# Pairwise bilinear interaction: transposes in feature pairs, x blocks by GpSimd's queue over 15 engines, and a last tile in six groups

## The chip, the cores and the metric

The kernel runs on one core of a Trainium2 chip. The metric is device time in microseconds (us) of one execution. TensorE (PE) multiplies, VectorE (DVE), ScalarE (ACT) and GpSimd (POOL) work elementwise, and SyncE (SP) only issues transfers. Sixteen DMA engines move data between device memory and the on-chip buffers; SP, ACT and POOL each put transfers on a queue of their own, and all three queues are served by the same sixteen engines.

## What is computed

There are 4096 batch rows, 32 features a row and 64 numbers a feature, all float32. For each of the 496 pairs of features i < j there is a 64 x 64 matrix. Feature i is multiplied by the pair's matrix, and the product elementwise by feature j:

```python
idx_i, idx_j = np.triu_indices(F, k=1)
vi = inputs[:, idx_i, :]
vj = inputs[:, idx_j, :]
vidots = jnp.einsum('bpd,pde->bpe', vi, W)
return vidots * vj
```

The output has 4096 x 496 x 64 numbers, 520 MB; x has 33.6 MB and w 8.1 MB.

## The kernel before

A *block* is 256 batch rows, two per partition; the 16 blocks give 32 *tiles* of 128 rows (`NB = 2` in a block). A tile's 496 pairs are cut into five *groups* (`bounds`, L45) of 90, 97, 99, 105 and 105 pairs. Each group is collected in an output buffer `ot` (three of them) and stored with one transfer on SP's queue (L266). A store has one row of up to 26,880 bytes per partition.

The multiplication needs x with the features' numbers on the partitions. `turn_x` (L138) makes a *run*: eight transposes on PE into a PSUM buffer, one of four, and one copy by ACT into `xT`. Transpose n takes the slots n and n + 1 of the block's buffer `xs`, so that feature n stands in the lower half of the partitions in one transpose and in the upper half in the next. There are four runs, or 32 transposes, per tile. Slot 0 of `xs` is a zero slot, written by a memset in `new_x` (L72).

The matrices are put in order (`order_w`) and transposed (`turn_w`) once, at the start, in chunks of 128 pairs; each chunk has a buffer `wT[c]` of its own. Two halves h of the output columns stand on two halves of the partitions, which is why each feature is wanted in both.

A *step* is one i and up to 16 of its j: for each half a matmul into a PSUM buffer (L244; two if the step crosses from one w chunk to the next), and one product. The product is DVE's (L261), or, for seven of the i, ACT copies PSUM to a buffer `tmp` (L258) and POOL multiplies (L259).

`sched` fixes the order of the steps: the first three tiles go group by group together, since w is still being prepared, and then tile after tile. Each engine works through its own instructions in program order. A run of transposes is placed `AHEAD` = 4 steps before its first use (L174 to L179).

The loads of x: blocks 0 and 1 at the start on SP's queue; block b + 1 at the seventh step of block b (`LATE`, L189 to L191). They wait until the buffer's old tile is done with. Most are one transfer on ACT's queue (`load_x`), which all sixteen DMA engines share. Blocks 4, 7, 10 and 13 (`loads[s] % 3 == 1`, L218) come by `load_fifteen` (L95): 120 of the 128 rows on POOL's queue in two transfers of half the features each, and the eight other rows on ACT's queue, five and three. After each of POOL's transfers stands a tiny one of a few bytes (`turn_engines`, L86)[...]. `turn_engines(5)` stands at the start and `turn_engines(11)` at the end (L270).

Of the kernel before, what the change touches and what calls it, by code (L numbers as in the profile page):

```python
# [8 lines left out]
F32 = mybir.dt.float32  # L9
# [3 lines left out]
def kernel(  # L13
# [16 lines left out]
    nc = tc.nc  # L30

    B, F, D = x.shape
    P = 128
    NB = 2
    assert 2 * D == P and B % (NB * P) == 0
    NBLK = B // (NB * P)
    NP = F * (F - 1) // 2
    E2 = D // 2
    BANK = 512
    CH = BANK // E2  # L40
    RUN = 2 * BANK // P
    p0 = [i * (F - 1) - i * (i - 1) // 2 for i in range(F)]


    bounds = [0, p0[3], p0[6] + CH, p0[11], p0[17], NP]  # L45
    groups = list(zip(bounds[:-1], bounds[1:]))
    cap = max(b - a for a, b in groups)

    aside = (1, 3, 5, 7, 9, 11, 13)

    cuts = [*range(0, NP, P), NP]
    wrows = list(zip(cuts[:-1], cuts[1:]))

    const = ctx.enter_context(tc.tile_pool(name="const", bufs=1))
    xpool = ctx.enter_context(tc.tile_pool(name="xpool", bufs=2))
    xtpool = ctx.enter_context(tc.tile_pool(name="xtpool", bufs=4))
    tpool = ctx.enter_context(tc.tile_pool(name="tpool", bufs=4))
    opool = ctx.enter_context(tc.tile_pool(name="opool", bufs=3))
    psum = ctx.enter_context(tc.tile_pool(name="psum", bufs=4, space=bass.MemoryType.PSUM))

    ident = const.tile([P, P], F32, tag="ident", name="ident")
    make_identity(nc, ident)

    xs = {}

    def rows_of(dram: bass.AP, blk: int) -> bass.AP:
        return dram[blk * NB * P : (blk + 1) * NB * P]

    def new_x(blk: int):

        xs[blk] = xpool.tile([P, 1 + NB * F, D], F32, tag="xs", name=f"xs_{blk}")
        nc.gpsimd.memset(xs[blk][:, 0, :], 0.0)  # L72

    def load_x(blk: int, eng, k0: int = 0, k1: int = NB):
        src = rows_of(x, blk).rearrange("(p k) f d -> p (k f) d", k=NB)
        eng.dma_start(out=xs[blk][:, 1 + k0 * F : 1 + k1 * F, :], in_=src[:, k0 * F : k1 * F, :])

# [3 lines left out]
    SWR = 120  # L81
# [4 lines left out]
    def turn_engines(k: int):  # L86
        n = k if k > 1 else 17
        c = used[0] % 8
        used[0] += 1
        src = x[: NB * n].rearrange("(p k) f d -> p k f d", k=NB)  # L90
        tc.keep_in_program_order(
            nc.gpsimd.dma_start(out=scratch[:n, :, c : c + 1], in_=src[:, :, 0, 0:1])  # L92
        )

    def load_fifteen(blk: int):  # L95
        rows = rows_of(x, blk).rearrange("(p k) f d -> p k f d", k=NB)
        dst = xs[blk][:, 1:, :].rearrange("p (k f) d -> p k f d", k=NB)
        for a, b in ((SWR, SWR + 5), (SWR + 5, P)):
            nc.scalar.dma_start(out=xs[blk][a:b, 1:, :], in_=rows[a:b].rearrange("p k f d -> p (k f) d"))
        for h in range(2):  # L100
            cut = slice(h * F // 2, (h + 1) * F // 2)
            tc.keep_in_program_order(
                nc.gpsimd.dma_start(out=dst[:SWR, :, cut, :], in_=rows[:SWR, :, cut, :])  # L103
            )
            turn_engines(1)


    wflat = w.rearrange("p d e -> p (d e)")
    raw, wT = {}, {}
    EU = 2 * BANK // P  # L110
    NU = E2 // EU

    def load_w(c: int, eng=nc.sync):

        a, b = wrows[c]
        pool, tag = ((opool, "ot"), (opool, "ot"), (const, "w3"), (const, "w3"))[c]
        raw[c] = pool.tile([P, D * D], F32, tag=tag, name=f"raw_{c}")
        eng.dma_start(out=raw[c][: b - a, :], in_=wflat[a:b])

    def order_w(c: int, k: int, copy):  # L120
        r = wrows[c][1] - wrows[c][0]
        rp = tpool.tile([P, EU, 2, D], F32, tag="tmp", name=f"rp_{c}_{k}")
        src = raw[c][:r, :].rearrange("p (d h e) -> p e h d", h=2, d=D)
        copy(rp[:r], src[:, k * EU : (k + 1) * EU])  # L124
        return rp

    def turn_w(c: int, k: int, rp, copy):
        r = wrows[c][1] - wrows[c][0]
        if c not in wT:
            wT[c] = const.tile([P, r, E2], F32, tag=f"w{c}", name=f"wT_{c}")  # L130
        pt = psum.tile([P, EU, P], F32, tag="ps", name=f"ptw_{c}_{k}")
        for n in range(EU):
            nc.tensor.transpose(  # L133
                pt[:, n, :r], rp[:r, n].rearrange("p h d -> p (h d)"), ident[:r, :r]
            )
        copy(wT[c][:, :, k * EU : (k + 1) * EU], pt[:, :, :r].rearrange("p e r -> p r e"))  # L136

    def turn_x(blk: int, k: int, q: int, copy):  # L138

        pt = psum.tile([P, RUN, P], F32, tag="ps", name=f"ptx_{blk}_{k}_{q}")  # L140
        for n in range(RUN):
            s = k * F + q * RUN + n
            nc.tensor.transpose(  # L143
                pt[:, n, :], xs[blk][:, s : s + 2, :].rearrange("p f d -> p (f d)"), ident
            )
        xT = xtpool.tile([P, RUN, P], F32, tag="xT", name=f"xT_{blk}_{k}_{q}")
        copy(xT, pt)  # L147
        return xT


    steps = [
        (g, i, c0, min(CH, F - 1 - i - c0))
        for i in range(F - 1)
        for c0 in range(0, F - 1 - i, CH)
        for g, (a, b) in enumerate(groups)
        if a <= p0[i] + c0 < b
    ]
    NS = len(steps)
    first = {}
    for s, (_, i, _, _) in enumerate(steps):  # L160
# [5 lines left out]
    NT = NBLK * NB  # L166
# [4 lines left out]
    place = {ts: n for n, ts in enumerate(sched)}  # L171


    AHEAD = 4  # L174
    due: dict = {}
    for t in range(NT):
        for q in range(F // RUN):
            at = place[t, first[q * RUN - 1] if q else 0] - AHEAD
            due.setdefault(max(0, at), []).append(("x", t // NB, t % NB, q))  # L179
    for c, orders, turns in (  # L180
# [9 lines left out]
    loads = {place[blk * NB, LATE]: blk + 1 for blk in range(2, NBLK - 1)}  # L190
# [12 lines left out]
    v, p, a = nc.vector.tensor_copy, nc.gpsimd.tensor_copy, nc.scalar.copy  # L203
    xT, rps = {}, {}
# [7 lines left out]
    ots = {}  # L212
    for s, (t, st) in enumerate(sched):
        blk, kt = divmod(t, NB)
        g, i, c0, m = steps[st]
        if s in loads:
            new_x(loads[s])
            if loads[s] % 3 == 1:  # L218
                load_fifteen(loads[s])
            else:  # L220
                load_x(loads[s], nc.scalar)
        for what, *args in due.get(s, ()):
            if what == "x":
                xT[tuple(args)] = turn_x(*args, a)
            elif what == "turn":
                turn_w(*args, rps.pop(tuple(args)), a)
            else:
                c, k = args
                rps[c, k] = order_w(c, k, (v, v, p, v)[c] if k % 2 == 0 else (v, v, p, a)[c])
                if (c, k) == (2, NU - 1):  # L230
                    load_w(3, nc.scalar)

        base, end = groups[g]
        pa = p0[i] + c0
        if pa == base:
            ots[t] = opool.tile([P, cap, D], F32, tag="ot", name=f"ot_{t}_{g}")
        ot = ots[t]
        ps = psum.tile([P, 2, CH, E2], F32, tag="ps", name=f"ps_{s}")
        for c, (lo, hi) in enumerate(wrows):
            lo, hi = max(pa, lo), min(pa + m, hi)  # L240
            if lo < hi:
                for h in range(2):
                    n = i + 1 - h
                    nc.tensor.matmul(  # L244
                        ps[:, h, lo - pa : hi - pa, :],
                        xT[blk, kt, n // RUN][h * D : (h + 1) * D, n % RUN, :],
                        wT[c][h * D : (h + 1) * D, lo - wrows[c][0] : hi - wrows[c][0], :],
                        start=True,
                        stop=True,
                    )  # L250
        o = pa - base
        j = 1 + kt * F + i + 1 + c0
        dst = ot[:, o : o + m, :].rearrange("p m (h e) -> p m h e", h=2)
        src = ps[:, :, :m, :].rearrange("p h m e -> p m h e")
        xj = xs[blk][:, j : j + m, :].rearrange("p m (h e) -> p m h e", h=2)
        if i in aside and c0 == 0 and s not in no_aside:
            tmp = tpool.tile([P, CH, 2, E2], F32, tag="tmp", name=f"tmp_{s}")
            nc.scalar.copy(tmp, src)  # L258
            nc.gpsimd.tensor_mul(dst, tmp, xj)  # L259
        else:  # L260
            nc.vector.tensor_mul(dst, src, xj)  # L261

        ends = (p0[2], end) if s < NS and (t, g) == (0, 0) else (end,)
        if pa + m in ends:
            n0 = p0[2] if len(ends) > 1 and pa + m == end else base
            nc.sync.dma_start(  # L266
                out=rows_of(out, blk).rearrange("(p k) n d -> p k n d", k=NB)[:, kt, n0 : pa + m, :],
                in_=ot[:, n0 - base : pa + m - base, :],
            )
    turn_engines(11)  # L270


# [25 lines left out]
```

## Time and profile before

| | |
|---|---|
| median of 9 runs (lowest, highest) | 1346.08 us (1345.64, 1346.99) |
| the profiled execution, its time | 1345.89 us |
| the profiled execution, its span, first to last instruction | 1344.1 us |
| busy: PE, DVE, ACT, POOL | 1166.7, 956.1, 374.0, 544.6 us |
| moved by DMA | 562.95 MB, mean 419 GB/s |
| queue of SP | 530.59 MB, 93.0% of sixteen engines' span |
| queue of ACT | 23.33 MB, 4.2% |
| queue of POOL | 7.88 MB, 1.5% |
| instruction fetches | 58 of 16 KB and 25 smaller packets, 0.3% |
| store of 105 pairs, issue to landing | 16.3 us (64 of them) |
| x load by ACT, issue to landing | 17.2 us (10) |
| x load by POOL, half of 120 rows, issue to landing | 31.4 us (8) |

The time outside the span is 1.77 us. A span is what the profile shows of one execution; the run's own time is what is compared between kernels. Busy shares are averages over the whole run, so a change in one stage has to be read from that stage.

### The profile page before, as it was taken

The numbers are of one execution on the slowest core, as the hardware profiler recorded it, in microseconds if no ns is written. First come the engines' busy times: TensorE is split into PE (matmuls) and PEld (weight loads), VectorE is DVE, ScalarE is ACT, GpSimd is POOL, SyncE is SP. The second block draws the span as 40 slices with busy tenths as digits, with TensorE's granted clock in tenths as the row PEclk, the third lists the DMA queues.
The fourth block names the chain that finished last, engine by engine and source line by source line (L and its number), as shares of the span: only waits on it lengthen the run. The fifth ranks groups of instructions, "written<-read, shape, count | busy, mean of one in ns | idle before, by whom it ended". The sixth has DMA issues, their size and how long they took to land.

```text
span 1344.1 us, 17902 instructions
## 1 busy us (share of the span) xinstructions
PE 1166.7 (87%) x7424; PEld 685.6 (51%) x7424; DVE 956.1 (71%) x1262; ACT 374.0 (28%) x367; POOL 544.6 (41%) x264
## 2 busy tenths in 40 slices
PE   6989889988799798888979988798988979988894
PEld 4555545544465454455545554454554545544552
DVE  4778767766677677776757777576776767767774
ACT  3442222323232232222322322222222323223321
POOL 1823434444243445333443534442444424344431
PEclk9989998999999899998989999899999999989997
DMA  9999999999999999999999999999999999999997
GB/s 378 370 431 424 424 428 433 428 417 430 422 431 422 426 430 407 426 422 430 429 424 420 411 425 430 420 428 419 421 419 415 428 427 427 421 433 421 421 414 320
DMA packets 28259, 562.95 MB, mean 419 GB/s; under 512 B 3457, under 2 KB 3457, under 8 KB 5505
## 3 DMA queue, kind: packets, MB, share of 16 engines
q1 hardware_dynamic: 24048, 530.59, 93.0%
q10 hardware_dynamic: 1632, 23.33, 4.2%
q0 software_dynamic: 2496, 7.88, 1.5%
q8 instruction: 58, 0.95, 0.3%
q14 instruction: 25, 0.20, 0.0%
HBM read 41.68 MB, written 520.09 MB: 418 GB/s over the span
## 4 chain that ended last, share of the span: by engine, by line
DMA 49%; PE 24%; DVE 17%; POOL 5%; issue 3%; ACT 1%; DVEq 0%; SPq 0%; POOLq 0%; ACTq 0%
DMA out_dram<-ot 48%; PE ps L244 19%; DVE ot L261 17%; POOL ot L259 4%; PE ptx L143 4%; PE ptw L133 1%; DMA raw<-in_L_rec_W_dram 1%; POOL scratch L92 1%; ACT tmp L258 0%; POOL xs L103 0%; DVE rp L124 0%; POOL rp L124 0%; DVEq L261 0%; ACT wT L136 0%; POOL xs L72 0%
## 5 line engine op out<-in xcount | busy, mean ns | idle before, releaser
L261 DVE TENSOR_TENSOR ot<-ps,xs 128x1024 f32<-128x1024 f32 (+15 forms) x1252 | 944.9, 808 | 355.9 <-DMA out_dram<-ot 185.0
L244 PE MATMUL ps<-wT,xT 64*128 64x512 f32 (+13 forms) x6272 | 1021.3, 469 | 125.0 <-DVE ot L261 113.8
L244 PEld LDWEIGHTS ps<-wT,xT 64*128 64x128 f32 x6272 | 558.1, 195 | 553.6 <-DVE ot L261 289.2
L259 POOL TENSOR_TENSOR ot<-tmp,xs 128x1024 f32<-128x1024 f32 x220 | 519.0, 2359 | 624.0 <-ACT tmp L258 453.3
L258 ACT COPY tmp<-ps 128x1024 f32<-128x1024 f32 x220 | 222.7, 1012 | 476.9 <-PE ps L244 433.0
L147 ACT COPY xT<-ptx 128x1024 f32<-128x1024 f32 x128 | 129.5, 1012 | 443.6 <-PE ptx L143 443.6
L143 PE MATMUL ptx<-ident,xs 128*128 128x128 f32 x1024 | 141.2, 281 | 30.7 <-DVE ot L261 21.9
L143 PEld LDWEIGHTS ptx<-ident,xs 128*128 128x128 f32 x1024 | 111.2, 142 | 76.9 <-issue 42.2
L72 POOL MEMSET xs<- 128x64 f32 x16 | 2.4, 151 | 147.3 <-DVE ot L261 147.3
L133 PE MATMUL ptw<-ident,rp 128*128 128x128 f32 (+1 forms) x128 | 19.3, 307 | 3.9 <-DVE rp L124 3.9
L133 PEld LDWEIGHTS ptw<-ident,rp 128*128 128x128 f32 (+1 forms) x128 | 16.3, 161 | 10.1 <-DVE rp L124 5.0
L136 ACT COPY wT<-ptw 128x1024 f32<-128x1024 f32 (+1 forms) x15 | 14.8, 984 | 21.1 <-PE ptw L133 18.2
L124 DVE COPY rp<-raw 128x1024 f32<-128x1024 f32 (+1 forms) x9 | 10.7, 1217 | 11.2 <-DMA raw<-in_L_rec_W_dram 11.2
L92 POOL DMA_DIRECT2D scratch<-in_r_inputs_dram x10 | 9.1, 908 | 0.2 <-issue 0.2
L124 POOL COPY rp<-raw 128x1024 f32<-128x1024 f32 x4 | 7.9, 1981 | 0.1
L124 ACT COPY rp<-raw 112x1024 f32<-112x1024 f32 (+1 forms) x3 | 5.9, 1959 | 4.3 <-POOL ot L259 2.5
L103 POOL DMA_DIRECT2D xs<-in_r_inputs_dram x8 | 6.0, 753 | 1.4 <-issue 1.4
L136 DVE COPY wT<-ptw 128x1024 f32<-128x1024 f32 x1 | 1.2, 1224 | 3.6 <-PE ptw L133 3.6
L147 ACT ACT_TABLE_LOAD x1 | 1.3, 1283 | 0.7 <-PEq L285 0.7
masks.py:197 POOL MEMSET ident<- 128x128 f32 x1 | 0.2, 205 | 0.3 <-POOLq L285 0.3
masks.py:199 POOL TENSOR_SCALAR_AFFINE_SELECT ident<-ident 128x128 f32<-128x128 f32 x1 | 0.3, 287 | 0.0
L285 POOL MEMSET const-float32-0.0<- 128x1 f32 x1 | 0.1, 93 | 0.3 <-issue 0.3
(3 smaller groups left out, 0.3 us busy)
## 6 DMA issues: line engine op xcount, KB each, us to landing
out_dram<-ot SPq DMA_DIRECT2D x64, 3360.0 KB, 16.3
out_dram<-ot SPq DMA_DIRECT2D x32, 3168.0 KB, 15.6
out_dram<-ot SPq DMA_DIRECT2D x32, 3104.0 KB, 17.0
out_dram<-ot SPq DMA_DIRECT2D x31, 2880.0 KB, 17.1
xs<-in_r_inputs_dram ACTq DMA_DIRECT2D x10, 2048.0 KB, 17.2
xs<-in_r_inputs_dram POOLq DMA_DIRECT2D x8, 960.0 KB, 31.4
raw<-in_L_rec_W_dram SPq DMA_DIRECT2D x3, 2048.0 KB, 17.3
xs<-in_r_inputs_dram SPq DMA_DIRECT2D x2, 1024.0 KB, 5.5
```

The source lines that it names most:

```text
L72: nc.gpsimd.memset(xs[blk][:, 0, :], 0.0)
L92: nc.gpsimd.dma_start(out=scratch[:n, :, c : c + 1], in_=src[:, :, 0, 0:1])
L103: nc.gpsimd.dma_start(out=dst[:SWR, :, cut, :], in_=rows[:SWR, :, cut, :])
L124: copy(rp[:r], src[:, k * EU : (k + 1) * EU])
L133: nc.tensor.transpose(pt[:, n, :r], rp[:r, n].rearrange("p h d -> p (h d)"), ident[:r, :r])
L136: copy(wT[c][:, :, k * EU : (k + 1) * EU], pt[:, :, :r].rearrange("p e r -> p r e"))
L143: nc.tensor.transpose(pt[:, n, :], xs[blk][:, s : s + 2, :].rearrange("p f d -> p (f d)"), ident)
L147: copy(xT, pt)
L244: nc.tensor.matmul(ps[:, h, lo - pa : hi - pa, :], xT[blk, kt, n // RUN][h * D : (h + 1) * D, n % RUN, :], wT[c][h * D : (h + 1) * D, lo - ...
L258: nc.scalar.copy(tmp, src)
L259: nc.gpsimd.tensor_mul(dst, tmp, xj)
L261: nc.vector.tensor_mul(dst, src, xj)
```

## The change

- `turn_x` makes four transposes per run rather than eight, each of two neighbouring features, and three copies by ACT: all four as they are, then each half of the partitions into the other half. A tile then has 16 transposes. The zero slot and its memset go. `xs` becomes one piece of 2048 numbers for each of the two rows with a gap of 16 numbers behind it.
- The first three w chunks share one buffer of 384 pairs, so a step that crosses pair 128 or 256 has one matmul per half.
- Runs are placed six steps before the first use of their features.
- `load_fifteen` is used for the blocks 3, 6, 9, 12 and 15. It sends 120 rows in one transfer of 8 KB pieces, then a tiny one, then the eight other rows in two transfers, all on POOL's queue.
- The last tile has six groups of 90, 97, 99, 55, 100 and 55 pairs. The fifth, of 100, is stored by POOL in two transfers, 120 rows and eight rows, with a gap of one pair between its halves of 50 in the output buffer. A tiny transfer `turn_engines(4)` follows it, in place of the one at the end.

```diff
-    RUN = 2 * BANK // P
+    RUN = 8
...
+    last = [*bounds[:4], p0[13] + CH, p0[21], NP]
+    last_groups = list(zip(last[:-1], last[1:]))
+    HALVED = 4
+    half = p0[17] - last[HALVED]
...
-        xs[blk] = xpool.tile([P, 1 + NB * F, D], F32, tag="xs", name=f"xs_{blk}")
-        nc.gpsimd.memset(xs[blk][:, 0, :], 0.0)
+        wide = xpool.tile([P, NB, F * D + 16], F32, tag="xs", name=f"xs_{blk}")
+        xs[blk] = wide[:, :, : F * D].rearrange("p k (f d) -> p k f d", d=D)
...
-        for a, b in ((SWR, SWR + 5), (SWR + 5, P)):
-            nc.scalar.dma_start(out=xs[blk][a:b, 1:, :], in_=rows[a:b].rearrange("p k f d -> p (k f) d"))
+        def part(ps: slice, fs: slice):
+            tc.keep_in_program_order(nc.gpsimd.dma_start(out=dst[ps, :, fs, :], in_=rows[ps, :, fs, :]))
+
+        part(slice(0, SWR), slice(0, F))
+        turn_engines(1)
         for h in range(2):
-            cut = slice(h * F // 2, (h + 1) * F // 2)
-            tc.keep_in_program_order(
-                nc.gpsimd.dma_start(out=dst[:SWR, :, cut, :], in_=rows[:SWR, :, cut, :])
-            )
-            turn_engines(1)
+            part(slice(SWR, P), slice(h * F // 2, (h + 1) * F // 2))
+
+    def store_fifteen(dram: bass.AP, ot: bass.AP):
+        dst = dram.rearrange("p (c n) d -> p c n d", c=2)
+        src = ot[:, : 2 * half + 2, :].rearrange("p (c n) d -> p c n d", c=2)[:, :, :half, :]
+        for rows in (slice(0, SWR), slice(SWR, P)):
+            tc.keep_in_program_order(nc.gpsimd.dma_start(out=dst[rows], in_=src[rows]))
...
-        if c not in wT:
-            wT[c] = const.tile([P, r, E2], F32, tag=f"w{c}", name=f"wT_{c}")
+        home, tag, n = (wrows[c][0], "w3", r) if c == 3 else (0, "w", wrows[3][0])
+        if home not in wT:
+            wT[home] = const.tile([P, n, E2], F32, tag=tag, name=f"wT_{home}")
...
-        pt = psum.tile([P, RUN, P], F32, tag="ps", name=f"ptx_{blk}_{k}_{q}")
-        for n in range(RUN):
-            s = k * F + q * RUN + n
+        pt = psum.tile([P, RUN // 2, P], F32, tag="ps", name=f"ptx_{blk}_{k}_{q}")
+        for u in range(RUN // 2):
+            f = q * RUN + 2 * u
             nc.tensor.transpose(
-                pt[:, n, :], xs[blk][:, s : s + 2, :].rearrange("p f d -> p (f d)"), ident
+                pt[:, u, :], xs[blk][:, k, f : f + 2, :].rearrange("p f d -> p (f d)"), ident
             )
-        xT = xtpool.tile([P, RUN, P], F32, tag="xT", name=f"xT_{blk}_{k}_{q}")
-        copy(xT, pt)
+        xT = xtpool.tile([P, 2, RUN // 2, P], F32, tag="xT", name=f"xT_{blk}_{k}_{q}")
+        copy(xT[:, 0], pt)
+        copy(xT[D:, 1], pt[:D])
+        copy(xT[:D, 1], pt[D:])
...
-    AHEAD = 4
+    AHEAD = 6
...
-            at = place[t, first[q * RUN - 1] if q else 0] - AHEAD
+            at = place[t, first[q * RUN]] - AHEAD
...
-            if loads[s] % 3 == 1:
+            if loads[s] % 3 == 0:
                 load_fifteen(loads[s])
...
-            nc.sync.dma_start(
-                out=rows_of(out, blk).rearrange("(p k) n d -> p k n d", k=NB)[:, kt, n0 : pa + m, :],
-                in_=ot[:, n0 - base : pa + m - base, :],
-            )
-    turn_engines(11)
+            dram = rows_of(out, blk).rearrange("(p k) n d -> p k n d", k=NB)[:, kt, n0 : pa + m, :]
+            if halved:
+                store_fifteen(dram, ot)
+                turn_engines(4)
+            else:
+                nc.sync.dma_start(out=dram, in_=ot[:, n0 - base : pa + m - base, :])
```

More of the change, by code (lines that the diff above doesn't have):

```diff
@@ L46 @@
     groups = list(zip(bounds[:-1], bounds[1:]))
+    last = [*bounds[:4], p0[13] + CH, p0[21], NP]
+    last_groups = list(zip(last[:-1], last[1:]))
+    HALVED = 4
+    half = p0[17] - last[HALVED]
+    assert last[HALVED + 1] == p0[17] + half
     cap = max(b - a for a, b in groups)
+    assert 2 * half + 1 < cap
     aside = (1, 3, 5, 7, 9, 11, 13)
@@ L69, in new_x @@
     def new_x(blk: int):
-        xs[blk] = xpool.tile([P, 1 + NB * F, D], F32, tag="xs", name=f"xs_{blk}")
-        nc.gpsimd.memset(xs[blk][:, 0, :], 0.0)
+        wide = xpool.tile([P, NB, F * D + 16], F32, tag="xs", name=f"xs_{blk}")
+        xs[blk] = wide[:, :, : F * D].rearrange("p k (f d) -> p k f d", d=D)
     def load_x(blk: int, eng, k0: int = 0, k1: int = NB):
-        src = rows_of(x, blk).rearrange("(p k) f d -> p (k f) d", k=NB)
-        eng.dma_start(out=xs[blk][:, 1 + k0 * F : 1 + k1 * F, :], in_=src[:, k0 * F : k1 * F, :])
+        src = rows_of(x, blk).rearrange("(p k) f d -> p k f d", k=NB)
+        eng.dma_start(out=xs[blk][:, k0:k1], in_=src[:, k0:k1])
     SWR = 120
@@ L96, in load_fifteen @@
         rows = rows_of(x, blk).rearrange("(p k) f d -> p k f d", k=NB)
-        dst = xs[blk][:, 1:, :].rearrange("p (k f) d -> p k f d", k=NB)
-        for a, b in ((SWR, SWR + 5), (SWR + 5, P)):
-            nc.scalar.dma_start(out=xs[blk][a:b, 1:, :], in_=rows[a:b].rearrange("p k f d -> p (k f) d"))
-        for h in range(2):
-            cut = slice(h * F // 2, (h + 1) * F // 2)
-            tc.keep_in_program_order(
-                nc.gpsimd.dma_start(out=dst[:SWR, :, cut, :], in_=rows[:SWR, :, cut, :])
-            )
-            turn_engines(1)
+        dst = xs[blk]
+        def part(ps: slice, fs: slice):
+            tc.keep_in_program_order(nc.gpsimd.dma_start(out=dst[ps, :, fs, :], in_=rows[ps, :, fs, :]))
+        part(slice(0, SWR), slice(0, F))
+        turn_engines(1)
+        for h in range(2):
+            part(slice(SWR, P), slice(h * F // 2, (h + 1) * F // 2))
[4 more added lines that the diff above has]
+            tc.keep_in_program_order(nc.gpsimd.dma_start(out=dst[rows], in_=src[rows]))
     wflat = w.rearrange("p d e -> p (d e)")
@@ L135, in turn_w, with steps_of @@
             )
-        copy(wT[c][:, :, k * EU : (k + 1) * EU], pt[:, :, :r].rearrange("p e r -> p r e"))
+        o = wrows[c][0] - home
+        copy(wT[home][:, o : o + r, k * EU : (k + 1) * EU], pt[:, :, :r].rearrange("p e r -> p r e"))
     def turn_x(blk: int, k: int, q: int, copy):
-        pt = psum.tile([P, RUN, P], F32, tag="ps", name=f"ptx_{blk}_{k}_{q}")
-        for n in range(RUN):
-            s = k * F + q * RUN + n
+        pt = psum.tile([P, RUN // 2, P], F32, tag="ps", name=f"ptx_{blk}_{k}_{q}")
+        for u in range(RUN // 2):
+            f = q * RUN + 2 * u
             nc.tensor.transpose(
-                pt[:, n, :], xs[blk][:, s : s + 2, :].rearrange("p f d -> p (f d)"), ident
+                pt[:, u, :], xs[blk][:, k, f : f + 2, :].rearrange("p f d -> p (f d)"), ident
             )
-        xT = xtpool.tile([P, RUN, P], F32, tag="xT", name=f"xT_{blk}_{k}_{q}")
-        copy(xT, pt)
-        return xT
[L151 to L157, printed above, removed]
+        xT = xtpool.tile([P, 2, RUN // 2, P], F32, tag="xT", name=f"xT_{blk}_{k}_{q}")
+        copy(xT[:, 0], pt)
+        copy(xT[D:, 1], pt[:D])
+        copy(xT[:D, 1], pt[D:])
+        return xT
+    def steps_of(groups):
+        return [
+            (g, i, c0, min(CH, F - 1 - i - c0))
+            for i in range(F - 1)
+            for c0 in range(0, F - 1 - i, CH)
+            for g, (a, b) in enumerate(groups)
+            if a <= p0[i] + c0 < b
+        ]
+    steps, last_steps = steps_of(groups), steps_of(last_groups)
     NS = len(steps)
@@ L214 @@
         blk, kt = divmod(t, NB)
-        g, i, c0, m = steps[st]
+        g, i, c0, m = (last_steps if t == NT - 1 else steps)[st]
         if s in loads:
             new_x(loads[s])
-            if loads[s] % 3 == 1:
+            if loads[s] % 3 == 0:
                 load_fifteen(loads[s])
@@ L231 @@
                     load_w(3, nc.scalar)
-        base, end = groups[g]
+        base, end = (last_groups if t == NT - 1 else groups)[g]
+        halved = (t, g) == (NT - 1, HALVED)
         pa = p0[i] + c0
@@ L238 @@
         ps = psum.tile([P, 2, CH, E2], F32, tag="ps", name=f"ps_{s}")
-        for c, (lo, hi) in enumerate(wrows):
-            lo, hi = max(pa, lo), min(pa + m, hi)
+        for lo, hi in ((0, wrows[3][0]), wrows[3]):
+            home, lo, hi = lo, max(pa, lo), min(pa + m, hi)
             if lo < hi:
                 for h in range(2):
-                    n = i + 1 - h
                     nc.tensor.matmul(
                         ps[:, h, lo - pa : hi - pa, :],
-                        xT[blk, kt, n // RUN][h * D : (h + 1) * D, n % RUN, :],
-                        wT[c][h * D : (h + 1) * D, lo - wrows[c][0] : hi - wrows[c][0], :],
+                        xT[blk, kt, i // RUN][h * D : (h + 1) * D, (i + h) % 2, i % RUN // 2, :],
+                        wT[home][h * D : (h + 1) * D, lo - home : hi - home, :],
                         start=True,
@@ L250 @@
                     )
-        o = pa - base
-        j = 1 + kt * F + i + 1 + c0
+        o = pa - base + (halved and pa - base >= half)
+        j = i + 1 + c0
         dst = ot[:, o : o + m, :].rearrange("p m (h e) -> p m h e", h=2)
         src = ps[:, :, :m, :].rearrange("p h m e -> p m h e")
-        xj = xs[blk][:, j : j + m, :].rearrange("p m (h e) -> p m h e", h=2)
+        xj = xs[blk][:, kt, j : j + m, :].rearrange("p m (h e) -> p m h e", h=2)
         if i in aside and c0 == 0 and s not in no_aside:
```

## The prediction

> **What bounds the kernel now.** I read the page's slices and queues first, then the stages, the waits, the end of the DMA, and the groups by shape.
>
> ```profile
> DMA  9999999999999999999999999999999999999997
> GB/s 378 370 431 424 424 428 433 428 417 430 422 431 422 426 430 407 426 422 430 429 424 420 411 425 430 420 428 419 421 419 415 428 427 427 421 433 421 421 414 320
> ...
> 33.00:100.00 67.00, 63.48 (x400) 38.61 (x398) 50.17 (x55) 29.29 (x28) 34.57 (x16) 0.95 0.97 400
> 100.00:1300.00 1200.00, 1057.91 (x6762) 617.53 (x6760) 870.03 (x1163) 325.89 (x322) 494.47 (x234) 0.96 1.00 424
> 1300.00:1345.00 45.00, 23.81 (x157) 14.43 (x154) 20.16 (x30) 6.08 (x6) 11.58 (x6) 0.78 0.79 335
> ```
>
> The last three lines are stages: length, busy PE, PEld, DVE, ACT and POOL, clock, DMA share, GB/s. Between 100 and 1300 us the 16 DMA engines are full; only the first 100 and the last 45 us are not. Bytes cannot be saved, so what can move is idle DMA time.
>
> ```profile
> DVE ot L261 <- DMA out_dram<-ot: 185.0, 84, 5.8
> POOL xs L72 <- DVE ot L261: 147.3, 14, 18.3
> ...
> 1318.81 7.86 DVE ot L261 x13
> 1326.67 0.13 DVEq L294
> ```
>
> The waits (total us, times, longest): VectorE waits 185.0 us for output buffers, 5.8 us a batch tile, so the multiplications are ahead of the DMA. The chain's end: the last group of 105 pairs is multiplied in 7.86 us and done at 1326.8.
>
> ```profile
> DMA  7079702220202000200020020002000000000000
> GB/s 323 0 323 1075 323 0 108 108 108 0 108 0 108 0 0 0 108 0 0 0 108 0 0 108 0 0 0 108 0 0 0 0 0 0 0 0 0 0 0 33
> ```
>
> This is the DMA view of 1334 to 1344 us, a slice each 0.25 us (a piece counts where it starts). From 1336 on one 26,880-byte piece starts about every microsecond: a single engine works alone. The packet records give the times: 13 engines finish the last store by 1336.0, others at 1336.8 and 1337.6, one at 1342.0; the span ends 2.1 us later. Sorted by store, the completions show this one engine, the laggard, 2.4 us behind at 178 us and 5 to 7 us behind through most of the later run. It falls back about 2.5% of the time, and catches up only while GpSimd loads x on 15 engines (7.2 to 3.5 us behind over the load at 517).
>
> Counting at each moment how many engines have no packet: 2.0 us before the first packet, 3.9 at 20 to 75 us, 5.9 between 100 and 1336 (2.5 of it after 1200), and 7.7 at the end, 5.6 of them waiting for the laggard. The idle time between 100 and 1336 comes when the laggard is over about 5.5 us late: it holds the output buffer that the next group needs.
>
> [...] a 26,880-byte piece takes 996 ns, 27.0 GB/s an engine, 432 for 16. [...] Here one stands out, and it falls back also when GpSimd transfers nothing. [...] this trace shows 5.4 us (issue 265.5, first 4 KB piece 270.9).
>
> **The change, part by part.**
>
> *Loads.* The packets cost 159 ns for 4 KB, 309 for 8 KB, 611 for 16 KB. A block loaded by ScalarE puts 8 x 611 = 4.89 us on each engine. Now: five blocks by GpSimd, 16 x 309 = 4.94 on 15 engines, and eight rows as 32 pieces of 4 KB over all 16, 0.32 each. Before: four blocks, 32 x 159 = 5.09 on 15 engines, none on the laggard[...]. Mean over engines: before 12 x 4.89 + 4 x 5.08 = 79.0 us, after 11 x 4.89 + 5 x 4.95 = 78.5: -0.4. Relief of the laggard against the others: before 4 x 5.09 = 20.4 us, after 5 x 4.94 = 24.7.
>
> What the laggard lost before is 20.4 (relief) + 6.2 (late at the end) + about 5.7 (the others idled) = 32 us, 6.05 per 246 us. After, the lag before each load (187, 431, 676, 923, 1169 us) should be 2.4, 3.5, 4.6, 5.7, 6.8, each load taking 4.9. Only the last two peaks pass 5.5, so of the 5.9 us about 1.2 stay: **-4.2**, keeping 0.5 for idleness of other causes (bounds -6 and 0).
>
> *Zero slot gone.* 16 memsets of 151 ns go. POOL's 147.3 us of waits stood before them with POOL otherwise idle; the load itself now waits for the same release, on ACT or POOL. Nothing. On POOL five blocks issue four DMAs each instead of four blocks with four (0.75 to 0.97 us each): 3.5 us once more, covered by POOL's 624 us idle; without cover the next product waits at most that.
>
> *Transposes and copies.*
>
> ```profile
> L258 ACT COPY tmp<-ps 128x1024 f32<-128x1024 f32 x220 | 222.7, 1012 | 476.9 <-PE ps L244 433.0 <-POOL ot L259 38.6
> L147 ACT COPY xT<-ptx 128x1024 f32<-128x1024 f32 x128 | 129.5, 1012 | 443.6 <-PE ptx L143 443.6
> L143 PE MATMUL ptx<-ident,xs 128*128 128x128 f32 x1024 | 141.2, 281 | 30.7 <-DVE ot L261 21.9 <-DMA xs<-in_r_inputs_dram 6.4
> ...
> L136 ACT COPY wT<-ptw 128x896 f32<-128x896 f32 x4 | 3.6, 906 | 8.9 <-PE ptw L133 5.9 <-DVE ot L261 2.9
> ```
>
> A run of eight transposes takes 1.09 us on PE; four take 0.55, so -70 us of PE in all, -2.2 a tile. ACT copies 1024 columns in 1012 ns and 896 in 906, so 512 in about 590; three are 1.76 us for one of 1.01: +0.75 a run, +96 in all, +3.0 a tile. Behind them on ACT stand copies into tmp, and POOL's products behind those. ACT idles over two thirds of the time and VectorE has 5.8 us a tile in hand, so in the middle this costs nothing. Six steps ahead instead of four leaves room for 1.76 us. The shared w buffer drops 256 matmul records at two crossings, same columns: nothing.
>
> In the first 75 us PE is the bound (95% busy from 33 to 100), and the 3.9 us of idle DMA is its. The three runs there before the first stores lose 1.6 us of PE, against 2.2 us more on ACT. I take **-1** (bounds -2.5 and +1.5).
>
> Fewer PE instructions mean fewer fetches (58 of 16 KB, 0.97 us each): -0.3 an engine. Loads, fetches and the tail's smaller pieces: **-0.7**.
>
> *The last tile*, on the clock of before, for the engines that lead. Pairs 90, 97, 99, then 55, 100 (GpSimd), 55. The lag there: 1.9 left after 1182, +3.2, about 5.1 instead of 6.4. Group 2 is transferred by 1319.2, the 55 by 1323.4 (14,080-byte rows, 8 in 4.2 us). The 100 pairs reuse the buffer of the 97, free on the leaders at 1311.5, on the laggard 5.1 later; nine products at about 0.8 us are 7.6 us, so done at 1324.8. GpSimd's store then needs 2.1 us (the tiny transfer at 1317.6 to its first packet) to 5.4 us (240 descriptors, as the loads); I take 5.4: 1330.2. The last 55 pairs are multiplied by 1329 and leave 0.85 us later (SP's first store: 27.64 to 28.48). So the leaders stand idle 1323.4 to about 1330, then have 4.2 + 7.7 us, seven of them one row of 0.95 us more: 1343.0. The laggard, relieved of seven of eight rows, is done near 1335. Against 1342.0: **+1** (bounds -2.5 and +2). That the new GpSimd transfers replace the closing tiny one is free: it was off the end.
>
> *Sum:* -4.2 -1 -0.7 +1 = -4.9 us. The profiled execution took 1345.89 (span 1344.12 and 1.77 around it); it lies 0.2 under the median, 1346.08. Forecast **1341.0**; own range 1339 to 1343.4.
>
> **Rivals.** Faster still: the last store starts after 2.1 us instead of 5.4 and the early runs pay fully, 3 to 4 us more: 1337.5. For it: HBM and the engines are idle then. Against it: the four loads all took about 5.4.
>
> No change: the idle time in the middle is not the laggard's but the group's own chain (release, 7 to 8 us of products, issue), and stays; with the tail's +1 and the other -1.7, near 1345. For it: stalls at 100 to 110 us, where the lag is small. Against it: under 0.1 us idle from 150 to 450, where the lag was mostly below 5.5.
>
> Slower: the three copies hold one of four PSUM buffers and ACT's queue, and PE and VectorE stop behind them. It decides once a run costs over 1.45 us of the chain (5.8 a tile in hand, four runs), more with PE's 0.55 back: about 2. That needs the half-width copies to cost a full 1.01 us each. Past it, each 0.1 us a run is 0.4 a tile and 13 us over 32 tiles; 0.35 a tile past it gives 11 - 5 = +6, 1352. Against: the slope of ACT's two widths.
>
> **How the numbers follow.** Forecast 0.42, faster still 0.22, no change 0.21, slower 0.15. A measurement of this kernel tells about 0.2% (2.7 us) from no change, so faster is 0.64, same 0.21, slower 0.15. The range 1335.5 to 1348.5 leaves out the slower case and a little of the fastest.
>
> **What would show it.** Right: the lag under 5.5 us until 900 us, idle engines under 2 us between 100 and 1300; no engine alone at the end, but a dip of all of them ahead of GpSimd's store; transposes 512, ACT copies near 590 ns. Wrong: the lag as large as before (the 15 engines are others), first GpSimd packets of the last store within 3 us, or VectorE's waits for the DMA gone and waits for PE or ACT in their place.

## The result and the profile after

The changed kernel takes 1355.04 us (median of 9 runs, 1352.88 to 1357.53), the kernel before 1346.23 in all its runs so far: ratio 1.0066, 95% interval 1.0057 to 1.0074. It is slower by 8.8 us, where 4.9 us less was forecast. The profiled execution took 1355.35 us with a span of 1353.6.

The page of the changed kernel, its slices and its DMA queues:

```profile
DMA  9999999999999999999999999999999999999995
GB/s 374 377 429 422 409 426 430 424 427 431 426 428 426 424 433 422 431 422 434 424 417 425 423 429 426 424 420 410 434 420 433 427 425 417 414 428 432 428 422 163
...
q1 hardware_dynamic: 24176, 527.31, 91.8%
q10 hardware_dynamic: 2576, 20.71, 3.8%
q0 software_dynamic: 2384, 13.78, 2.9%
```

The middle looks as before. The last slice fell from 320 to 163 GB/s. The stages of the same kernel (length; busy PE, PEld, DVE, ACT, POOL; clock; DMA share; GB/s) show what happens in it:

```profile
100.00:1300.00 1200.00, 1044.89 (x6076) 551.96 (x6072) 868.20 (x1164) 414.05 (x561) 495.38 (x224) 0.94 1.00 425
1320.00:1326.00 6.00, 5.82 (x38) 3.38 (x36) 4.90 (x6) 1.74 (x3) 0.82 (x2) 0.91 0.14 58
1326.00:1336.00 10.00, 2.57 (x24) 1.50 (x20) 3.19 (x9) 0.00 (x0) 1.12 (x2) 0.77 0.98 216
1336.00:1352.00 16.00, 0.00 (x0) 0.00 (x0) 0.00 (x0) 0.00 (x0) 0.00 (x0) 0.50 0.59 183
```

Two things are to be seen. From 1320 to 1326 us the DMA engines have almost nothing to do (share 0.14). That was in the forecast. From 1326 to 1336 they are all at work (0.98), yet move 216 GB/s, half of the 425 that the same share gives in the middle. That was not. In the packet records GpSimd's 12,800-byte pieces of the fifth group take 945 ns (median), many between 940 and 1000. At the 27 GB/s an engine of every other store (26,880 bytes in 996 ns) they would take 479 ns, and some do: eight of the 124 that started before 1334.4 us, and many of the later ones. That 15 engines carry the 120 rows is seen in the semaphore records of that transfer: of its 16 landing marks one comes at 1327.4 us, 0.9 us after the first piece starts, and the other fifteen from 1339.3 us on.

The end of the chain and GpSimd's own timeline:

```profile
1314.71 0.30 DVE ot L282
...
1324.00 5.06 DVE ot L282 x10
1329.06 0.13 DVEq L316
...
1310.24 2.34 POOL L280 TENSOR_TENSOR ot<-tmp,xs 128x1024 f32<-128x1024 f32 x1 [0.63 <-ACT tmp L279]
1325.18 1.35 POOL L118 DMA_DIRECT2D out_dram<-ot  x2 [12.60 <-DVE ot L282]
1326.53 0.59 POOL L99 DMA_DIRECT2D scratch<-in_r_inputs_dram  x1
```

VectorE is done with everything at 1329.1; the last piece lands at 1351.0. So 22 us of transfers stand after the last product, where the kernel before had 15 (1326.8 to 1342.0).

The groups on ScalarE and PE, for the copies that the change multiplied:

```profile
L163 ACT COPY xT<-ptx 128x512 f32<-128x512 f32 x128 | 74.9, 585 | 330.7 <-PE ptx L159 330.7
L159 PE MATMUL ptx<-ident,xs 128*128 128x128 f32 x512 | 85.7, 291 | 11.2 <-DMA xs<-in_r_inputs_dram 8.6
L165 ACT COPY xT<-ptx 64x512 f32<-64x512 f32 x128 | 74.5, 582 | 1.5
L164 ACT COPY xT<-ptx 64x512 f32<-64x512 f32 x128 | 73.9, 577 | 1.5
```

They cost what was worked out, 580 ns each and 94 us more in all than the one copy of before, and VectorE still waits for output buffers above all:

```profile
DVE ot L282 <- DMA out_dram<-ot: 204.7, 94, 6.3
```

So nothing here points to the copies. When I count the moments at which an engine has no packet, the middle even gained: between 100 and 1320 us 3.5 us of idleness instead of 5.8. The store of the 97 pairs of the last tile is through on the leading engines at 1307.3 us instead of 1311.5, that of the 99 at 1314.9 instead of 1319.7.

### The profile page after: what moved, and what is told of

The parts are those of the page before. It is cut to its first block, busy times and chain, and to the rows that moved or that the text cites. A ratio compares the mean times of both kernels' runs of the same rounds, so it can differ in the third digit from the quotient of the medians.

```text
span 1353.6 us, 16680 instructions
## 1 busy us (share of the span) xinstructions
PE 1149.1 (85%) x6656; PEld 611.6 (45%) x6656; DVE 954.6 (71%) x1262; ACT 467.6 (35%) x623; POOL 544.4 (40%) x254
## 4 chain that ended last, share of the span: by engine, by line
DMA 55%; PE 23%; DVE 12%; POOL 4%; issue 2%; ACT 1%; SPq 0%; DVEq 0%; POOLq 0%; ACTq 0%
DMA out_dram<-ot 53%; PE ps L265 21%; DVE ot L282 12%; POOL ot L280 4%; PE ptx L159 2%; DMA xs<-in_r_inputs_dram 2%; ACT tmp L279 1%; PE ptw L147 1%; DVE rp L137 0%; POOL rp L137 0%; ACT xT L163 0%; ACT xT L164 0%; DVEq L282 0%; POOL xs L107 0%; ACT xT L165 0%
## 5 line engine op out<-in xcount | busy, mean ns | idle before, releaser
L265 PE MATMUL ps<-wT,xT 64*128 64x512 f32 (+13 forms) x6016 | 1056.2, 492 | 163.7 <-DVE ot L282 158.5
L265 PEld LDWEIGHTS ps<-wT,xT 64*128 64x128 f32 x6016 | 540.2, 197 | 619.8 <-DVE ot L282 365.2
L163 ACT COPY xT<-ptx 128x512 f32<-128x512 f32 x128 | 74.9, 585 | 330.7 <-PE ptx L159 330.7
L159 PE MATMUL ptx<-ident,xs 128*128 128x128 f32 x512 | 85.7, 291 | 11.2 <-DMA xs<-in_r_inputs_dram 8.6
L159 PEld LDWEIGHTS ptx<-ident,xs 128*128 128x128 f32 x512 | 54.8, 143 | 85.4 <-DVE ot L282 59.4
L165 ACT COPY xT<-ptx 64x512 f32<-64x512 f32 x128 | 74.5, 582 | 1.5
L164 ACT COPY xT<-ptx 64x512 f32<-64x512 f32 x128 | 73.9, 577 | 1.5
L107 POOL DMA_DIRECT2D xs<-in_r_inputs_dram x15 | 9.5, 636 | 0.0
L99 POOL DMA_DIRECT2D scratch<-in_r_inputs_dram x7 | 6.2, 890 | 0.3 <-issue 0.3
```

What stands on the lines that cost most here:

```text
L107: tc.keep_in_program_order(nc.gpsimd.dma_start(out=dst[ps, :, fs, :], in_=rows[ps, :, fs, :]))
L159: nc.tensor.transpose(pt[:, u, :], xs[blk][:, k, f : f + 2, :].rearrange("p f d -> p (f d)"), ident)
L163: copy(xT[:, 0], pt)
L164: copy(xT[D:, 1], pt[:D])
L165: copy(xT[:D, 1], pt[D:])
L265: nc.tensor.matmul(ps[:, h, lo - pa : hi - pa, :], xT[blk, kt, i // RUN][h * D : (h + 1) * D, (i + h) % 2, i % RUN // 2, :], wT[home][h * ...
```

## The experiments

My new theory (A): the last tile costs more than the whole loss, and the rest gains. Within it, theory P: the rows are at fault. A store that is cut by rows runs at about half the rate (here 216 of 425 GB/s), whatever its queue and the number of its engines. That is a guess from these two figures; what in the hardware would do it, no run shows. Rivals: the loss is in the copies, the w buffer or the loads (B), in GpSimd's queue (Q), or in transfers over 15 engines as such (R).

**The last tile undone.** The changed kernel with five groups in the last tile, all by SP, and the closing tiny transfer back at the end:

```diff
-        g, i, c0, m = (last_steps if t == NT - 1 else steps)[st]
+        g, i, c0, m = steps[st]
...
-        base, end = (last_groups if t == NT - 1 else groups)[g]
-        halved = (t, g) == (NT - 1, HALVED)
+        base, end = groups[g]
...
```

> The changed kernel with the last tile as before: five groups, all stored by SP, the closing tiny transfer at the end. Theory A (the last tile costs all of the loss; loads, transposes and w buffer gain about 4.8 us, as the stores up to the last tile's third show): about 1341 us, the laggard alone at the end, 6 us late. Theory B (three copies by ACT, shared w buffer or the loads lose time as well): 1347 us or more.

1342.53 us (10 runs), ratio to before 0.9974 (0.9965 to 0.9984): 3.6 us faster than before. The view of its DMA from 1330 to 1340 us, a slice each 0.25 us, has the single late engine again:

```profile
DMA  7099702520022002000200020002000000000000
GB/s 323 0 753 645 323 0 108 215 108 0 0 108 108 0 0 108 0 0 0 108 0 0 0 108 0 0 0 108 0 0 0 0 0 0 0 0 0 0 0 33
```

Theory A holds: against this kernel the new last tile costs 12.5 us. The gain of the rest is a little under what was expected.

**The last tile alone.** The kernel before, with only the six groups and GpSimd's two transfers added:

> The kernel before with only the new last tile (six groups, the 100 pairs by GpSimd, 120 and 8 rows). Theory A: 12 to 15 us over before, 1358 to 1361 us, 12,800-byte pieces near 950 ns. Theory B: under 1350.

1358.61 us (4 runs), ratio 1.0094 (1.0079 to 1.0109): +12.5 us. Its 12,800-byte pieces took 948 ns (median). Nothing else of the change is needed for the loss.

**Six groups, all by SP.** The changed kernel, with the fifth group as an ordinary store:

```diff
-            if halved:
-                store_fifteen(dram, ot)
-                turn_engines(4)
-            else:
-                nc.sync.dma_start(out=dram, in_=ot[:, n0 - base : pa + m - base, :])
+            nc.sync.dma_start(out=dram, in_=ot[:, n0 - base : pa + m - base, :])
+    turn_engines(11)
```

> The changed kernel with the six groups kept and the group of 100 pairs stored by SP in one transfer of 128 rows. If the six groups alone leave the engines idle for some 7 us ahead of the 100 pairs, and the rest of the loss is GpSimd's store: 1341 to 1344 us, pieces of 25,600 bytes at about 950 ns. If the six groups are the whole loss: 1353 to 1355.

1343.27 us (20 runs), ratio 0.9978 (0.9971 to 0.9985). The six groups do leave the engines idle before the fifth (4.5 us between 1320 and 1336, averaged over the engines), but it hardly tells: 0.7 us over the five groups, within the intervals. In the gap the late engine catches up, so that at the end all 16 finish within 0.9 us instead of one 6.3 us late. The loss lies in the store itself.

**128 rows by GpSimd.** The changed kernel, with one transfer for the fifth group (here and in the next two the closing tiny transfer is `turn_engines(11)` instead of 4; it stands behind the store):

```diff
-        for rows in (slice(0, SWR), slice(SWR, P)):
-            tc.keep_in_program_order(nc.gpsimd.dma_start(out=dst[rows], in_=src[rows]))
+        tc.keep_in_program_order(nc.gpsimd.dma_start(out=dst, in_=src))
```

> The changed kernel with GpSimd's store of the 100 pairs as one transfer of all 128 rows in the same 12,800-byte pieces. Theory P [...]: pieces of 479 ns, 1342 to 1345 us. Theory Q (GpSimd's queue reads SBUF slowly whatever the rows): pieces stay near 950 ns, 1350 us or more.

1343.62 us (20 runs), ratio 0.9980 (0.9973 to 0.9987); pieces of 484 ns. The stage of that store:

```profile
1328.00:1338.00 10.00, 2.40 (x22) 1.50 (x20) 3.02 (x9) 0.00 (x0) 0.38 (x1) 0.70 1.00 419
```

The same queue, the same pieces, full share, and 419 GB/s. Q falls.

**120 and 8 rows by SP.** The two transfers as they are, on SP's queue:

```diff
-            tc.keep_in_program_order(nc.gpsimd.dma_start(out=dst[rows], in_=src[rows]))
+            nc.sync.dma_start(out=dst[rows], in_=src[rows])
```

> The changed kernel with the same two transfers of the 100 pairs (120 rows, eight rows, pieces of 12,800 bytes) issued by SP instead of GpSimd. Theory P [...]: pieces near 950 ns as with GpSimd's queue, about 1353 to 1356 us. Theory Q (it is GpSimd's queue): 479 ns, 1341 to 1344 us.

1355.35 us (4 runs), ratio 1.0069 (1.0053 to 1.0086); pieces of 980 ns:

```profile
1328.00:1338.00 10.00, 3.04 (x26) 1.81 (x24) 3.74 (x10) 0.00 (x0) 0.00 (x0) 0.77 0.97 224
```

The loss follows the rows and not the queue. Two more things are in these packet records. One engine does run at full rate: from 1328.4 us on its pieces take 487, 499, 496, 500, 486, 482 and 479 ns, one right behind the other, while those of the other engines take about 1 us. And the eight rows left over, 120 to 127, are slower still: their 16 pieces took 1.76 us on average, the longest 3.8. Why the one is spared and the others are slower was not shown.

**64 and 64 rows by SP.** The last kernel with the cut at row 64 instead of 120, so that 16 engines take part:

```diff
-        for rows in (slice(0, SWR), slice(SWR, P)):
+        for rows in (slice(0, P // 2), slice(P // 2, P)):
```

> The changed kernel with the 100 pairs stored by SP as rows 0 to 63 and rows 64 to 127, pieces of 12,800 bytes, 16 engines each. Theory P [...]: pieces near 950 ns, 1351 to 1356 us. Theory R (only a transfer over 15 engines is slow): 479 ns, 1341 to 1345 us.

1351.74 us (4 runs), ratio 1.0042 (1.0028 to 1.0056); pieces of 1001 ns:

```profile
1327.00:1337.00 10.00, 2.49 (x24) 1.51 (x20) 3.10 (x9) 0.00 (x0) 0.00 (x0) 0.72 1.01 218
```

All 16 engines are busy (share 1.01) and move 218 GB/s. None runs at full rate here: of the first 128 pieces only one, which started late, took less than 0.85 us. R falls: a store over 16 engines loses half its rate too, once it is cut by rows. This kernel takes 3.6 us less than that of the 120 rows; here no eight rows are left over and no engine sits out, but what each of the two is worth was not taken apart.

That a store cut by rows runs at half rate is shown: 224 and 218 GB/s, where the same pieces in one transfer of 128 rows moved 419. What in the hardware does it is not. In all these stores the same rows of the output buffer go to the same rows of `out`, so the side that is read is not separated from the side that is written. And the x loads of 120 rows show no halving: in the kernel of "The last tile undone" each of their 8 KB pieces overlapped with seven to nine others on average, and 98% still took about the 309 ns of an undisturbed piece. So what is shown holds for the stores of the last tile alone.

**Where the gain comes from.** The kernel before with other blocks on 15 engines, nothing else:

```diff
-            if loads[s] % 3 == 1:
+            if loads[s] % 3 == 0:
```

> The kernel before with the blocks 3, 6, 9, 12, 15 instead of 4, 7, 10, 13 loaded over 15 engines, nothing else. If the 3.6 us that the changed kernel gains with its old last tile come from the relief of the slow engine: 1342 to 1343.5 us. If they come from the transposes and the shared w buffer: 1345.5 to 1347.

1344.12 us (20 runs), ratio 0.9985 (0.9978 to 0.9992): 1.7 us faster. That is half of the 3.6 and between the two expectations. The choice of the blocks gives about half of the gain; the other half is shared by the transposes, the w buffer and the new form of the loads, which were not taken apart.

**No relief.** The changed kernel with its old last tile and every block over all 16 engines (`if False:` in the same place):

> The changed kernel with the last tile as before and every x block on ACT's queue over all 16 engines. If one engine has some 32 us more to do than the others and holds the output buffers, nothing relieves it: the other engines idle 15 us or more and the time is 1355 to 1366 us. If the loads over 15 engines matter little: 1342 to 1346.

1354.68 us (4 runs), ratio 1.0063 (1.0049 to 1.0078): 12.2 us over five relieved blocks, and just under the expected range. Between 100 and 1336 us the other engines idle for 11.6 us, and one engine ends 6.3 us after the leaders. The late engine is real, and to relieve it pays; but it has 18 us more to do than the rest here (11.6 and 6.3), not 32.

**Seven blocks.** The changed kernel with its old last tile and the blocks 3, 5 .. 15 over 15 engines (`% 2 == 1`):

> The last tile as before, and seven blocks (3, 5 .. 15) instead of five loaded over 15 engines. If the one slow engine still sets the end and holds buffers, two blocks more relieve it by 9.9 us: its 6 us at the end go and most of the 3 us of idle engines between 100 and 1320 too: 1335 to 1338 us, against 1342.5 with five. If other engines set the end: 1341 to 1344.

1338.05 us (5 runs), ratio 0.9947 (0.9934 to 0.9960), the fastest here: 8 us under before and 17 under the changed kernel. Idle time between 100 and 1320 us fell to 1.8 us. But the 6 us at the end, on which the expectation also counted, did not go: in the profiled execution (1341.28 us, the slowest of the five) one engine still ends 5.9 us late. Its 26,880-byte pieces take the ordinary 996 ns from 1205 us to the end. In the kernel before and without relief the last engine's pieces cost 3 to 4% more between loads until VectorE is done with its products, and 996 ns only after that. So the late one here is not the slow one. Which it is, I have not settled.

**Seven blocks in the kernel before.**

> The kernel before with the seven odd blocks 3 to 15 instead of 4, 7, 10, 13 loaded over 15 engines, nothing else. If the relief of the slow engine is what counts: 1339.5 to 1342 us, 1.5 to 3 us over the same seven blocks with the new transposes (1338.05). If the new transposes and loads in 8 KB pieces do most of it: 1343.5 to 1346.

1341.80 us (5 runs), ratio 0.9961 (0.9948 to 0.9975): within the upper end of the expectation, though 3.75 us over the seven blocks with the new transposes, where at most 3 were expected. The two profiled executions are only 2.1 us apart (1343.39 and 1341.28). In them the packets' time per engine is 1334.1 against 1329.8 us, but the first has less idle time between 100 and 1336 us, 2.3 against 4.5 us. Of these 4.3 us, 2.8 are x packets on GpSimd's and ScalarE's queues (78.6 against 75.8 us): 4 KB pieces took 171 ns on average, two of them 342, where an 8 KB piece took 312. Another 0.4 us are instruction fetches. So the form of the loads is a likely part of the 3.75 us, but no run has it alone.

## Why the prediction was wrong

**The step that failed** is in the part on the last tile: "then have 4.2 + 7.7 us". The 7.7 us priced the 16 pieces of 12,800 bytes by the rate of an engine alone (479 ns), and took that rate for any choice of rows. The pieces took 840 ns on average, 13.4 us an engine for the 256 pieces; spread unevenly and alternating with the last group's, they ended at 1351.0. The term was +1 us and measured +12.5, twice: 1355.04 against 1342.53, and 1358.61 against 1346.12. The range held no bound for it, because I bounded the start of GpSimd's store from both sides and its rate not at all. The rival for a slower kernel named another place, the copies; it fell.

**Right in it:** the idle engines ahead of that store. 6.8 us were forecast, and the leaders had 7.4 (1319.1 to 1326.5). The sum was right by two errors that cancel. GpSimd's store began 1.35 us after its issue, not 5.4. The group was ready late instead, because the laggard was 6.8 us behind at the 97 pairs and not 5.1, and the group's products took 10.4 us (1314.7 to 1325.1) and not 7.6; PE's clock was 0.52 from 1314 to 1320.

**Loads and the laggard, -4.2:** mechanism shown, size too large. Idle time between 100 and 1320 us fell from 5.8 to 3.25 us with the old last tile, -2.6. I took all that the laggard loses to be 32 us, with the full 20.4 of relief counted in. Without relief the loss is 18 us, and five relieved blocks gave back 12.2 us, or 2.4 a load instead of 4.9. After the loads two or three other engines are the late ones, 3 to 5 us behind, and the buffers then wait for them; why these fall behind is open.

**Start, -1:** not there. The idle time from 20 to 100 us was 3.9 us before and between 4.1 and 7.1 in the kernels with the new transposes.

**Packets' time, -0.7:** 1330.6 us an engine before, 1329.0 with the old last tile, -1.6.

**Copies, transposes, memsets, the w buffer at nothing:** no cost of them shows. ACT copies of 512 columns took 577 to 586 ns (590 forecast), and with the same blocks on 15 engines the kernel with the new transposes is 1.6 us (five blocks) and 3.75 us (seven) faster than the one without, though the intervals of the ratios overlap a little each time.

Without the last tile the forecast was -5.9 us and the measured change -3.6.

## What to carry to other kernels

A piece's time on one engine was its price only in stores of all 128 rows. Before a store is cut by rows, measure one such store, and look in the trace for a full DMA share at half the GB/s (here 0.98 at 216, against 1.00 at 425). To take load off a slow DMA engine, leave it out of loads, which here alternated with the stores and cost about the same per byte (8 KB in 309 ns, 26,880 bytes in 996), and keep the stores at 128 rows: the 100 pairs took 1343.3 and 1343.6 us in one transfer of 128 rows, and 1351.7 us or more when cut. And when a change has a new kind of transfer, bound its rate as well as its start.

## What the runs showed of the hardware

- Stores of 120 rows over 15 engines, or of 64 rows over 16, moved 216 to 224 GB/s at a DMA share of 0.97 to 1.01; a store of 128 rows in the same pieces moved 419. SP's and GpSimd's queue made no difference (pieces of 980 and 945 ns, 1355.35 and 1355.04 us).
- GpSimd's loads of 120 rows showed no such halving: 8 KB pieces took 319 ns on average beside SP's stores, 309 at the median, with about four of them under way at a time. Whether loads alone would be halved was not tried.
- GpSimd's first packet came 1.35 us after the issue of the last tile's store, when the engines were nearly idle. With full engines it came 5.2 to 5.5 us after it in the four loads of the kernel before, and 3.6 to 4.9 us in the five loads, of half as many pieces, of the changed kernel with its old last tile.
- One of the 16 engines needs about 3.4% more per store piece, with and without GpSimd transfers beside it (3.7% in the kernel before, 3.3% without relief, both between loads). After VectorE's last product (1326.8 us in the kernel before, 1335.9 without relief) its pieces too take 996 ns, from about 1 us later on. What slows it is open.
